# A Perceiver kernel on one core: the last experts' input made apart from its block, the last recurrence in other memory, and its end in two halves

## Chip, core and metric

The kernel runs on one core of one Trainium2 chip. The metric is the device time of one execution in microseconds (us), lower is better. The engines are named as in the profile: PE is TensorE (PEld its weight loads), DVE is VectorE, ACT is ScalarE, POOL is GpSimd, SP is SyncE, whose queue issues nearly all DMAs of the part in question. Each engine works through its own list of instructions in order. The lists are made when the kernel is built, and they interleave parts that the program writes one after the other: in the trace the input of block 2's experts is made in the middle of `recur(3)`, which stands before it in the program. So the order of the program works as a priority, not as a sequence.

## What is computed

64 sequences of 32 tokens with 256 channels (2048 tokens, float32) go through two layers, each with an attention part, a recurrent part and a feed-forward part, each added to the token. The change touches the last two parts of the second layer: the recurrence (a selective state-space model with 512 channels and 16 states) and the dense mixture of 8 experts.

```python
def _L1_attn_ref(x, ...):                      # x is normalised by the caller
    residual = x
    xz = x @ in_proj_w.T + in_proj_b
    x_main, z = jnp.split(xz, 2, axis=-1)
    xc = silu(causal_conv4(x_main) + conv_b)
    ssm = xc @ x_proj_w.T + x_proj_b
    B_param, C_param = ssm[..., :16], ssm[..., 16:32]
    delta = softplus(ssm[..., -1:])
    A = -jnp.exp(A_log)
    def step(h, ts):
        dt, B_t, C_t, x_t = ts
        h = jnp.exp(A[None] * dt[:, :, None]) * h + dt[:, :, None] * B_t[:, None, :] * x_t[:, :, None]
        return h, jnp.einsum('bdn,bn->bd', h, C_t) + D * x_t
    _, ys = lax.scan(step, h0, xs)
    y = (ys * silu(z)) @ out_proj_w.T + out_proj_b
    r = y + residual
    return layernorm(r) * ln_gamma + ln_beta

def _L1_ffn_ref(x, ...):                       # x is normalised by the caller
    logits = rms(xf @ gate_w.T + gate_b) * rms_w
    g = top_1(softmax(logits / 0.5))
    norm_g = g / (g + 1e-06)
    h = gelu(einsum('nd,edh->neh', xf, w1) + b1)
    y = einsum('neh,ehd->ned', h, w2) + b2     # all 8 experts, every token
    return (y * norm_g[:, None, None]).sum(axis=1)

x = x + _L1_attn_ref(_layernorm(x), ...)
x = x + _L1_ffn_ref(_layernorm(x), ...)
```

## The kernel before

The tokens stand in four blocks of 512, `k.x[0..3]`, each as four tiles of 128 tokens by 256 channels. `layers` (from L1233) runs six stages over them. The second layer's parts are `s3`, attention, by tiles of 128 tokens, called as `on(n, ...)`; `ahead`, `gates` and `recur` of `_stage4`, the recurrence, by blocks; and `s5` of `_stage5`, the experts, by blocks. Towards its end the program reads: attention for the last tiles (`on(6)`, `on(2)`, `on(4)`) with `ahead(2)`, `recur(1)` and `gates(2)` among them, then `s5(0)`, `ahead(3)`, `recur(2)`, `gates(3)`, `s5(1)`, `recur(3)`, `s5(2)`, `s5(3)`.

**The recurrence.** `ahead(b)` normalises the block, transposes it into `xT` (tag `xT4`, one buffer), makes the convolved channels `xc` (later `y`), sends B, C and the step through DRAM (`rows`) and turns the step into `dt` by a softplus of nine operations on ACT and DVE (L1059 to L1067). `gates(b)` makes `zs`, the gate, from the same `xT4` (L1075). `recur(b, v)` first multiplies `y` by `dt` (`dtx`, half on DVE, half on POOL, L1083). Then it goes over 16 states; for each, SP fetches one row of B and one of C to all partitions (`bc`, 512 KB, L1089), and for each half of the channels POOL makes `g` = dtx times B (L1092), ACT the decay `h` = exp(A dt) into a bank of PSUM (tag `h`, two banks, L1096), DVE runs the scan in place (L1097) and multiplies by C into `hc` (L1098), and POOL adds `hc` to `y` (L1103). `bc`, `g` and `hc` have two buffers each in the pool `wk`. After the states POOL multiplies `y` by the gate (L1106); then, tile by tile, the residual and `bout` are put into `xe` (L1110, L1111), PE projects `y` (`outps`, in the same two banks, L1114), DVE adds, and after all four tiles come the moments and a reciprocal root (`_rsqrt`: three operations on DVE, L84 to L87, and 12 Newton steps on POOL, L89 to L92), and gamma, beta and the sum into `x` on POOL (L1119 to L1121).

**The experts.** `block(b)` of `_stage5` has a head and a body. The head (L1152 to L1192): moments, `_rsqrt`, normalised tiles `xn5` (one buffer), transposes into `t_ps` (tag `u`, the one bank that `up` also uses), a copy to `xT5` (one buffer), the gate's logits `lg_ps` (L1166, same bank), and a softmax that ends in `gt`. The body (L1194 on) goes over 32 slices of 128 hidden channels, four for each expert: `up` (L1207, two matmuls into the one bank), an evacuation with the bias on ACT (L1209), and after four of them one gelu over the expert's `hid` (L1211, two buffers); the products with the second weights, `acc` (L1215), run one expert behind, into two banks. In the trace one matmul of this kind leaves two records, so a slice is four records of `up` and four of `acc`. Each expert's weights come on SP's queue (L1202, L1203, 512 KB each, two buffers each). At the end `acc` goes to `res` (L1220, in the buffer of `xT5`), is transposed back (`rT`, L1227, in the bank of `up`), multiplied by the gate and added to `x` into `o5` (L1228, in the buffer of `xn5`), and written out in two halves (L1230).

PSUM has eight banks here: two for attention, two `h`, one for projections (`psp`), one `u` (`psu`), two `acc`.

Of the kernel before, what the change touches and what calls it, by code (L numbers as in the profile page):

```python
# [8 lines left out]
F32 = mybir.dt.float32  # L9
# [6 lines left out]
P = 128  # L16
# [59 lines left out]
def _rsqrt(k, out, parts, tag, pool=None):  # L76


    nc, pool, f = k.nc, pool or k.small, out.shape[-1]
    n = out.shape[0]  # L80
    v, r, t = (pool.tile([P, f], F32, name=f"rs_{q}", tag=f"rs_{q}{tag}")[:n] for q in "vrt")
    at = 0
    for in_, scale, eps in parts:
        nc.vector.tensor_scalar(v[:, at : at + in_.shape[-1]], in_, scale, eps, ALU.mult, ALU.add)  # L84
        at += in_.shape[-1]
    nc.vector.tensor_scalar(r.bitcast(I32), v.bitcast(I32), 1, None, ALU.logical_shift_right)
    nc.vector.tensor_scalar(r.bitcast(I32), r.bitcast(I32), -1.0, 1597463007.0, ALU.mult, ALU.add)  # L87
    for step in range(3):
        nc.gpsimd.tensor_tensor(t, r, r, ALU.mult)  # L89
        nc.gpsimd.tensor_tensor(t, t, v, ALU.mult)  # L90
        nc.gpsimd.tensor_scalar(t, t, -0.5, 1.5, ALU.mult, ALU.add)
        nc.gpsimd.tensor_tensor(out if step == 2 else r, r, t, ALU.mult)  # L92
# [13 lines left out]
def _stats(k, tiles, tag, pool=None):  # L106

    mv = _moments(k, tiles, tag, pool)
    rstd = (pool or k.small).tile([P, len(tiles)], F32, name="rstd", tag=f"rstd{tag}")
    _rsqrt(k, rstd, [(mv[:, :, 1], 1.0, LN_EPS)], tag, pool)  # L110
    return mv, rstd
# [859 lines left out]
def _stage4(k, w, wk):  # L971
# [105 lines left out]
    def recur(b, v):  # L1077
        xs = [k.x[b][:, j, :] for j in range(4)]
        dt, y = v.dt, v.y
        dtx = wk.tile([P, C, BT], F32, name="dtx", tag="dtx", bufs=1)  # L1080
# [6 lines left out]
        for n in range(N):  # L1087
            bc = wk.tile([P, 2, BT], F32, name="bc", tag="bc", bufs=2)
            nc.sync.dma_start(bc, bc_rows[n].partition_broadcast(P))  # L1089
            for c2 in range(0, C, 2):  # L1090
                g = wk.tile([P, 2, BT], F32, name="g", tag="g", bufs=2)
                nc.gpsimd.tensor_tensor(g, dtx[:, c2 : c2 + 2], bc[:, 0:1, :].to_broadcast([P, 2, BT]), ALU.mult)  # L1092
                hc = wk.tile([P, 2, BT], F32, name="hc", tag="hc", bufs=2)
                for c in range(2):
                    h = ph([P, BT], "h")
                    nc.scalar.activation(h, dt, AF.Exp, scale=A[:, c2 + c, n : n + 1])  # L1096
                    nc.vector.tensor_tensor_scan(h, h, g[:, c, :], 0.0, ALU.mult, ALU.add)  # L1097
                    nc.vector.tensor_tensor(hc[:, c, :], h, bc[:, 1, :], ALU.mult)  # L1098
                if n == 0:

                    for c in range(c2, c2 + 2):
                        nc.scalar.activation(y[:, c, :], y[:, c, :], AF.Copy, scale=_chan(k, "L1_attn_D", c))
                nc.gpsimd.tensor_tensor(y[:, c2 : c2 + 2], y[:, c2 : c2 + 2], hc, ALU.add)  # L1103

        for c2 in range(0, C, 2):
            nc.gpsimd.tensor_tensor(y[:, c2 : c2 + 2], y[:, c2 : c2 + 2], v.zs[:, c2 : c2 + 2], ALU.mult)  # L1106
        xn = wk.tile([P, 4, D], F32, name="xe4", tag="hc", bufs=2)
# [9 lines left out]
        for j in range(4):  # L1117
            _norm(k, xn[j], xn[j], mv, rstd, j)
            nc.gpsimd.tensor_tensor(xn[j], xn[j], gamma, ALU.mult)  # L1119
            nc.gpsimd.tensor_tensor(xs[j], xs[j], beta, ALU.add)  # L1120
            nc.gpsimd.tensor_tensor(xs[j], xs[j], xn[j], ALU.add)  # L1121

# [6 lines left out]
def _stage5(k, w, out):  # L1129
# [12 lines left out]
    def ps(shape, name):  # L1142
        return k.psu.tile(shape, F32, name=name, tag="u")
# [7 lines left out]
    def block(b):  # L1151
        xs = [k.x[b][:, j, :] for j in range(4)]  # L1152
        mv, rstd = _stats(k, xs, "5")
        xT = k.wk5.tile([P, 2, BT], F32, name="xT5", tag="xT5", bufs=1)
        for j2 in range(0, 4, 2):
            xn = k.wk5.tile([P, 2, D], F32, name="xn5", tag="xn5", bufs=1)
            t_ps = ps([P, 2, 2 * P], "t_ps")
            for j in range(2):
                _norm(k, xn[:, j, :], xs[j2 + j], mv, rstd, j2 + j)
                for c in range(2):  # L1160
                    nc.tensor.transpose(t_ps[:, c, j * P : (j + 1) * P], xn[:, j, c * P : (c + 1) * P], k.ident)
            nc.scalar.copy(xT[:, :, j2 * P : (j2 + 2) * P], t_ps)
        lg_ps = ps([P, 4, E], "lg_ps")
# [28 lines left out]
        nc.vector.tensor_tensor(gt, gt, gn, ALU.mult)  # L1192

        acc = [k.psacc.tile([P, BT], F32, name="acc", tag="acc") for _ in range(2)]  # L1194
# [23 lines left out]
        res = k.wk5.tile([P, 2, BT], F32, name="res", tag="xT5", bufs=1)  # L1218
        for o in range(2):
            nc.scalar.activation(res[:, o, :], acc[o], AF.Identity, bias=b2s[:, o : o + 1])  # L1220
        for j2 in range(0, 4, 2):
            rT = ps([P, 2, D], "rT")
            t = k.wk5.tile([P, 2, D], F32, name="o5", tag="xn5", bufs=1)
# [8 lines left out]
    return block  # L1232


def layers(k, out):
# [11 lines left out]
    left0, left, right, right2 = ExitStack(), ExitStack(), ExitStack(), ExitStack()  # L1247
    k.lent = False
    with left0:
# [11 lines left out]
        k.wk3 = pool("wk3", 2)  # L1261
# [7 lines left out]
    with right, left:  # L1269
# [26 lines left out]
        s5 = _stage5(k, w5, out)  # L1296
        k.wk5 = pool("wk5", 2)
        on(6, True)
# [5 lines left out]
        s5(0)  # L1304
# [3 lines left out]
        s5(1)  # L1308
        recur(3, v[3])
        s5(2)  # L1310
        s5(3)
# [81 lines left out]
```

## Time and profile before

| what | value |
|---|---|
| median of 3 runs | 2078.18 us (2077.95 to 2079.32) |
| the profiled execution | 2077.47 us |
| its span, first to last instruction | 2075.5 us |
| mean granted TensorE clock | 0.826 |
| attention's last softmax row (L891) | starts at 1585.8 us |
| recurrences, start of the first g and of the last (L1092) | 773.2 and 997.2; 1123.4 and 1329.6; 1414.2 and 1638.8; 1704.8 and 1855.7 us |
| experts, block 0 | first up 1094.1, res 1410.0 us |
| block 1 | first up 1463.5, res 1734.2 us |
| block 2 | first up 1767.4, res 1925.4 us |
| block 3 | first up 1943.1, res 2064.7 us |

All times in the lower part are counted from the start of the span. The costliest groups of the page (line, engine, operation, tiles, shape, count, then busy time and mean length in ns, then the idle time just before them and what ended most of it) are those of the recurrence and the experts:

```profile
L1092 POOL TENSOR_TENSOR g<-dtx,bc 128x1024 f32<-128x1024 f32 x128 | 300.5, 2354 | 132.5 <-DVE h L1097 68.1
L1097 DVE TENSOR_TENSOR_SCAN h<-h,g 128x512 f32<-128x512 f32 x256 | 307.4, 1218 | 62.9 <-ACT h L1096 43.1
L1103 POOL TENSOR_TENSOR xc<-xc,hc 128x1024 f32<-128x1024 f32 x128 | 301.3, 2358 | 36.8 <-DVE hc L1098 22.9
L1207 PE MATMUL up<-xT,w 128*128 128x512 f32 x512 | 283.6, 670 | 38.9 <-ACT hid L1209 38.3
L1215 PE MATMUL acc<-hid,w 128*128 128x512 f32 x512 | 259.5, 630 | 27.2 <-ACT hid L1211 27.2
L1209 ACT ACTIVATE hid<-up,chan 128x512 f32<-128x512 f32 x128 | 87.4, 683 | 142.6 <-PE up L1207 142.4
```

The mean matmul length here is that of overlapping instructions and of two clocks; where PE is dense and the granted clock is 1.0, four records of `up` take 1.72 us in the chain.

### The profile page before, as it was taken

Reading aid. Unit: us, or ns where it says so; the run is one execution under the profiler, and the core shown is the slowest. Engines: PE = TensorE matmul, PEld = TensorE weight load, DVE = VectorE, ACT = ScalarE, POOL = GpSimd, SP = SyncE. Lnnn points to the kernel's source line nnn. Section 1 sums busy time; section 2 is a strip of 40 time slices with the busy share of each in tenths; the row PEclk is TensorE's granted clock in tenths of the full one; section 3 lists DMA queues with packets and bytes.
Section 4 is the critical chain, followed back from the end, with each engine's and each line's share of the span. In section 5 each row is a group of like instructions: output and inputs, shape, how many; then the busy total and the mean of one; then the engine's idle time right before and its main releaser. Section 6 shows DMA issues by size and latency. Waiting matters only on the chain. (4 is left out here: it accounts for less than half of the span.)

```text
span 2075.5 us, 20210 instructions
## 1 busy us (share of the span) xinstructions
PE 1616.5 (78%) x6323; PEld 823.7 (40%) x6323; DVE 1365.0 (66%) x2419; ACT 985.7 (47%) x2142; POOL 1074.2 (52%) x1221
## 2 busy tenths in 40 slices
PE   4676957669979888766888888787698674779798
PEld 3333524325645433433444344344343231234343
DVE  4488586765574559889765788757897758772100
ACT  3454343304535264444447676556476464553232
POOL 5444646413241316676633777734777759893000
PEclk9686867879989997555788899896699886999799
DMA  7654233200001012121101233111222113222121
GB/s 231 228 190 143 92 100 115 82 22 21 21 21 43 20 35 64 31 62 51 41 31 58 81 102 102 40 45 54 61 69 70 55 47 92 80 81 72 40 81 41
DMA packets 88378, 151.25 MB, mean 73 GB/s; under 512 B 7740, under 2 KB 52300, under 8 KB 86224
## 3 DMA queue, kind: packets, MB, share of 16 engines
q1 hardware_dynamic: 85428, 148.75, 23.6%
q10 hardware_dynamic: 2844, 1.22, 0.3%
q8 instruction: 50, 0.82, 0.2%
q14 instruction: 56, 0.46, 0.1%
HBM read 139.03 MB, written 10.92 MB: 72 GB/s over the span
## 5 line engine op out<-in xcount | busy, mean ns | idle before, releaser
L1092 POOL TENSOR_TENSOR g<-dtx,bc 128x1024 f32<-128x1024 f32 x128 | 300.5, 2354 | 132.5 <-DVE h L1097 68.1
L1097 DVE TENSOR_TENSOR_SCAN h<-h,g 128x512 f32<-128x512 f32 x256 | 307.4, 1218 | 62.9 <-ACT h L1096 43.1
L1103 POOL TENSOR_TENSOR xc<-xc,hc 128x1024 f32<-128x1024 f32 x128 | 301.3, 2358 | 36.8 <-DVE hc L1098 22.9
L1207 PE MATMUL up<-xT,w 128*128 128x512 f32 x512 | 283.6, 670 | 38.9 <-ACT hid L1209 38.3
L1215 PE MATMUL acc<-hid,w 128*128 128x512 f32 x512 | 259.5, 630 | 27.2 <-ACT hid L1211 27.2
L1096 ACT ACTIVATE h<-dt,A 128x512 f32<-128x512 f32 x256 | 172.9, 693 | 156.0 <-DVE hc L1098 155.8
L891 ACT ACTIVATE p<-sc,nm 128x256 f32<-128x256 f32 x256 | 117.7, 472 | 120.9 <-DVE nm L887 107.0
L1098 DVE TENSOR_TENSOR hc<-h,bc 128x512 f32<-128x512 f32 x256 | 169.5, 678 | 2.7 <-POOL xc L1103 1.0
L880 PE MATMUL sc<-kT,qm 32*128 32x256 f32 x512 | 145.1, 492 | 29.6 <-DVE od L920 21.4
L89 POOL TENSOR_TENSOR rs_t<-rs_r 128x4 f32<-128x4 f32 (+4 forms) x174 | 39.2, 228 | 246.5 <-DVE rs_r L87 233.1
L1207 PEld LDWEIGHTS up<-xT,w 128*128 128x128 f32 x512 | 98.1, 208 | 163.5 <-issue 87.1
L630 PE MATMUL weps<-we,xT 128*128 128x512 f32 x256 | 148.3, 705 | 14.8 <-DVE x L626 7.4
L1215 PEld LDWEIGHTS acc<-hid,w 128*128 128x128 f32 x512 | 98.7, 202 | 148.4 <-issue 102.9
L1209 ACT ACTIVATE hid<-up,chan 128x512 f32<-128x512 f32 x128 | 87.4, 683 | 142.6 <-PE up L1207 142.4
L906 PE MATMUL pt_ps<-ident,p 128*128 128x128 f32 x512 | 96.3, 322 | 36.6 <-ACT p L891 27.2
L880 PEld LDWEIGHTS sc<-kT,qm 32*128 32x128 f32 x512 | 85.5, 229 | 80.8 <-DVE od L920 35.0
L1228 DVE SCALAR_TENSOR_TENSOR o<-rT,gt,x 128x256 f32<-128x256 f32 x16 | 7.6, 477 | 164.7 <-PE rT L1227 158.4
L885 DVE TENSOR_REDUCE nm<-sc 128x2 f32<-128x512 f32 x128 | 86.0, 682 | 35.4 <-PE sc L880 34.8
L906 PEld LDWEIGHTS pt_ps<-ident,p 128*128 128x128 f32 x512 | 66.7, 162 | 90.3 <-ACT p L891 48.5
L908 ACT COPY pt<-pt_ps 128x512 f32<-128x512 f32 x128 | 74.4, 586 | 59.0 <-PE pt_ps L906 58.4
L530 POOL TENSOR_TENSOR kk<-kk 128x512 f32<-128x512 f32 x32 | 34.1, 1072 | 110.0 <-ACT kk L529 107.2
L247 POOL TENSOR_TENSOR cT<-cT,scb 128x2056 f32<-128x2056 f32 x16 | 73.2, 4575 | 27.6 <-PE sc L258 15.6
(390 smaller groups left out, 3203.3 us busy)
## 6 DMA issues: line engine op xcount, KB each, us to landing
bc<-rows SPq DMA_DIRECT2D x64, 512.0 KB
w<-in_L_ffn_w_dram SPq DMA_DIRECT2D x64, 512.0 KB
cT<-in_ctxT_dram SPq DMA_DIRECT2D x16, 1028.0 KB
cq<-cq SPq DMA_DIRECT2D x32, 514.0 KB
cn<-in_ctx_dram SPq DMA_DIRECT2D x64, 256.0 KB
scb<-scales SPq DMA_DIRECT2D x16, 514.0 KB
kb<-steps SPq DMA_DIRECT2D x16, 514.0 KB
x<-in_x_dram SPq DMA_DIRECT2D x4, 512.0 KB
```

Source lines behind the costliest of these rows:

```text
L630: nc.tensor.matmul(ps, xT[:, c, r], we[:, c, e : e + 2, :], start=c == 0, stop=c == 1)
L880: nc.tensor.matmul(sc[h][:, f, :], qm[r, e + f].rearrange("p l n g -> p (l n g)"), kTs[e][r, f, :], start=True, stop=True,)
L891: nc.scalar.activation(w_[:, f, h - h0, :], sc[h][:, f, :], AF.Exp, bias=nm[:, e + f, h : h + 1], accum_out=sm[:, e + f, h : h + 1],)
L906: nc.tensor.transpose(pt_ps[:, h, m, :], ws[e, hp][:, f, h, m * P : (m + 1) * P], k.ident)
L1092: nc.gpsimd.tensor_tensor(g, dtx[:, c2 : c2 + 2], bc[:, 0:1, :].to_broadcast([P, 2, BT]), ALU.mult)
L1096: nc.scalar.activation(h, dt, AF.Exp, scale=A[:, c2 + c, n : n + 1])
L1097: nc.vector.tensor_tensor_scan(h, h, g[:, c, :], 0.0, ALU.mult, ALU.add)
L1098: nc.vector.tensor_tensor(hc[:, c, :], h, bc[:, 1, :], ALU.mult)
L1103: nc.gpsimd.tensor_tensor(y[:, c2 : c2 + 2], y[:, c2 : c2 + 2], hc, ALU.add)
L1207: nc.tensor.matmul(u, w1[e][:, c, q * P : (q + 1) * P], xT[:, c, :], start=c == 0, stop=c == 1)
L1209: nc.scalar.activation(hid[e][:, q, :], u, AF.Identity, bias=b1)
L1215: nc.tensor.matmul(acc[o], w2[e][:, q, o * P : (o + 1) * P], hid[e][:, q, :], start=n == H, stop=n == E * H + H - 1)
```

## The change

Five things change.

1. `block` is split into `head(b, mem)`, which makes `xT`, the logits and the gate, and `block(b, v)`, the body. The head's `t_ps` and `lg_ps` move from the bank of `up` to the two banks of tag `h`. Its `xT` comes from a pool that is handed in: `in5` (one buffer) for blocks 0 and 1, `late` (two buffers) for blocks 2 and 3.
2. The heads get places of their own in the program: head 0 before `on(6)`, head 1 right after the body of block 0, head 2 after `gates(3)` and before the body of block 1, head 3 after `recur(3)` and before the body of block 2.
3. The pool of attention, `wk3`, gets a stack of its own (`right3`) and is closed after the last `on`; `late` is opened in its place. `recur(3)` takes `bc`, `g` and `hc` from `late`, with three buffers each instead of two.
4. For block 3 alone, `recur` makes the residual (norm, `bout`, and beta into `x`) at its start, in the buffer of `xT4`, and ends in two halves of two tiles (`end`): four matmul groups into one bank, one add over both tiles, moments, `_rsqrt` with its Newton steps on DVE instead of POOL, and two DVE operations for each tile in place of one on DVE and two on POOL. Head 3 also takes its moments and reciprocal root by pairs, on DVE.
5. A block's `res` and output go to one tile `last` in a buffer of `hid`, with a place for each half of the output.

```diff
-def _rsqrt(k, out, parts, tag, pool=None):
+def _rsqrt(k, out, parts, tag, pool=None, eng=None):
...
+    eng = eng or nc.gpsimd
...
-        nc.gpsimd.tensor_tensor(t, r, r, ALU.mult)
+        eng.tensor_tensor(t, r, r, ALU.mult)
...
-    def recur(b, v):
+    def recur(b, v, mem=None):
         xs = [k.x[b][:, j, :] for j in range(4)]
         dt, y = v.dt, v.y
+        if b == NBLK - 1:
+            xn = residual(v, xs)
+        own, more = (mem, 1) if mem else (wk, 0)
...
-            bc = wk.tile([P, 2, BT], F32, name="bc", tag="bc", bufs=2)
+            bc = own.tile([P, 2, BT], F32, name="bc", tag="bc", bufs=2 + more)
...
-                g = wk.tile([P, 2, BT], F32, name="g", tag="g", bufs=2)
+                g = own.tile([P, 2, BT], F32, name="g", tag="g", bufs=2 + more)
...
-                hc = wk.tile([P, 2, BT], F32, name="hc", tag="hc", bufs=2)
+                hc = own.tile([P, 2, BT], F32, name="hc", tag="hc", bufs=2 + more)
...
+        if b == NBLK - 1:
+            for j2 in range(0, 4, 2):
+                end(v, xs, xn, j2)
+            return
...
+    def residual(v, xs):
+        xn = wk.tile([P, 4, D], F32, name="xr4", tag="xT4", bufs=1)
+        for j in range(4):
+            _norm(k, xn[:, j, :], xs[j], v.mv, v.rstd, j)
+            nc.gpsimd.tensor_tensor(xn[:, j, :], xn[:, j, :], bout, ALU.add)
+            nc.gpsimd.tensor_tensor(xs[j], xs[j], beta, ALU.add)
+        return xn
+
+    def end(v, xs, xn, j2):
+        ps = ph([P, 2, D], "outps")
+        for j in range(2):
+            for c in range(C):
+                at = slice((j2 + j) * P, (j2 + j + 1) * P)
+                nc.tensor.matmul(ps[:, j, :], v.y[:, c, at], wout[:, c, :], start=c == 0, stop=c == C - 1)
+        t = xn[:, j2 : j2 + 2, :]
+        nc.vector.tensor_tensor(t, ps, t, ALU.add)
+        mv, rstd = _stats(k, [t[:, j, :] for j in range(2)], "4e", wk, nc.vector)
+        for j in range(2):
+            x = xs[j2 + j]
+            nc.vector.scalar_tensor_tensor(t[:, j, :], t[:, j, :], mv[:, j, 0:1], gamma, ALU.subtract, ALU.mult)
+            nc.vector.scalar_tensor_tensor(x, t[:, j, :], rstd[:, j : j + 1], x, ALU.mult, ALU.add)
...
-    def block(b):
-        xs = [k.x[b][:, j, :] for j in range(4)]
-        mv, rstd = _stats(k, xs, "5")
-        xT = k.wk5.tile([P, 2, BT], F32, name="xT5", tag="xT5", bufs=1)
+    def head(b, mem):
+        v = Ctx()
+        xs = v.xs = [k.x[b][:, j, :] for j in range(4)]
+        pairs = b == NBLK - 1
+        if not pairs:
+            mv, rstd = _stats(k, xs, "5")
+        xT = v.xT = mem.tile([P, 2, BT], F32, name="xT5", tag="xT5")
...
-            t_ps = ps([P, 2, 2 * P], "t_ps")
+            t_ps = k.psh.tile([P, 2, 2 * P], F32, name="t_ps", tag="h")
+            if pairs:
+                mv, rstd = _stats(k, xs[j2 : j2 + 2], "5e", k.wk5, nc.vector)
...
-        lg_ps = ps([P, 4, E], "lg_ps")
+        lg_ps = k.psh.tile([P, 4, E], F32, name="lg_ps", tag="h")
...
+        v.gt = gt
+        return v
+
+    def block(b, v):
+        xs, xT, gt = v.xs, v.xT, v.gt
...
-        res = k.wk5.tile([P, 2, BT], F32, name="res", tag="xT5", bufs=1)
+        last = k.wk5.tile([P, 4, BT], F32, name="last", tag="hid")
+        res, outs = last[:, 0:2, :], last[:, 2:4, :].rearrange("p a (b d) -> p (a b) d", d=D)
...
-            t = k.wk5.tile([P, 2, D], F32, name="o5", tag="xn5", bufs=1)
+            t = outs[:, j2 : j2 + 2, :]
...
-        k.wk3 = pool("wk3", 2)
+        k.wk3 = opened(right3, "right")("wk3", 2)
...
-        s5 = _stage5(k, w5, out)
+        head, s5 = _stage5(k, w5, out)
         k.wk5 = pool("wk5", 2)
+        in5 = pool("in5", 1)
+        f = {0: head(0, in5)}
         on(6, True)
         v[2] = ahead(2)
         recur(1, v[1])
         gates(v[2])
         on(2, False)
         on(4, True, last=True)
-        s5(0)
+
+        right3.close()
+        late = opened(right, "right")("late", 2)
+        s5(0, f[0])
+        f[1] = head(1, in5)
         v[3] = ahead(3)
         recur(2, v[2])
         gates(v[3])
-        s5(1)
-        recur(3, v[3])
-        s5(2)
-        s5(3)
+        f[2] = head(2, late)
+        s5(1, f[1])
+        recur(3, v[3], late)
+        f[3] = head(3, late)
+        s5(2, f[2])
+        s5(3, f[3])
```

More of the change, by code (lines that the diff above doesn't have):

```diff
@@ L88, in _rsqrt @@
     for step in range(3):
-        nc.gpsimd.tensor_tensor(t, r, r, ALU.mult)
-        nc.gpsimd.tensor_tensor(t, t, v, ALU.mult)
-        nc.gpsimd.tensor_scalar(t, t, -0.5, 1.5, ALU.mult, ALU.add)
-        nc.gpsimd.tensor_tensor(out if step == 2 else r, r, t, ALU.mult)
+        eng.tensor_tensor(t, r, r, ALU.mult)
+        eng.tensor_tensor(t, t, v, ALU.mult)
+        eng.tensor_scalar(t, t, -0.5, 1.5, ALU.mult, ALU.add)
+        eng.tensor_tensor(out if step == 2 else r, r, t, ALU.mult)
 def _moments(k, tiles, tag, pool=None):
@@ L103, in _moments, with _stats @@
     return mv
-def _stats(k, tiles, tag, pool=None):
+def _stats(k, tiles, tag, pool=None, eng=None):
     mv = _moments(k, tiles, tag, pool)
     rstd = (pool or k.small).tile([P, len(tiles)], F32, name="rstd", tag=f"rstd{tag}")
-    _rsqrt(k, rstd, [(mv[:, :, 1], 1.0, LN_EPS)], tag, pool)
+    _rsqrt(k, rstd, [(mv[:, :, 1], 1.0, LN_EPS)], tag, pool, eng)
     return mv, rstd
@@ L1149, in _stage5 @@
     nc.vector.tensor_copy(b2s, bs_ps)
-    def block(b):
-        xs = [k.x[b][:, j, :] for j in range(4)]
-        mv, rstd = _stats(k, xs, "5")
-        xT = k.wk5.tile([P, 2, BT], F32, name="xT5", tag="xT5", bufs=1)
+    def head(b, mem):
[5 more added lines that the diff above has]
+        xT = v.xT = mem.tile([P, 2, BT], F32, name="xT5", tag="xT5")
         for j2 in range(0, 4, 2):
             xn = k.wk5.tile([P, 2, D], F32, name="xn5", tag="xn5", bufs=1)
-            t_ps = ps([P, 2, 2 * P], "t_ps")
+            t_ps = k.psh.tile([P, 2, 2 * P], F32, name="t_ps", tag="h")
+            if pairs:
+                mv, rstd = _stats(k, xs[j2 : j2 + 2], "5e", k.wk5, nc.vector)
             for j in range(2):
-                _norm(k, xn[:, j, :], xs[j2 + j], mv, rstd, j2 + j)
+                _norm(k, xn[:, j, :], xs[j2 + j], mv, rstd, j if pairs else j2 + j)
                 for c in range(2):
@@ L1230, in block @@
             nc.sync.dma_start(out[at : at + 2 * P, :].rearrange("(j p) d -> p j d", p=P), t)
-    return block
+    return head, block
 def layers(k, out):
@@ L1246, in layers @@
     psum = dict(space=bass.MemoryType.PSUM)
-    left0, left, right, right2 = ExitStack(), ExitStack(), ExitStack(), ExitStack()
+    left0, left, right, right2, right3 = (ExitStack() for _ in range(5))
     k.lent = False
@@ L1268, in layers @@
         s1(NBLK - 1)
-    with right, left:
+    with right, right3, left:
         pool = opened(left, "left")
```

## The prediction

> **What bounds the kernel now.** I read the engine shares, then the 40 slices, the chain that ended last, and at last tables by stage for the stretches where the chain shows a gap on TensorE.
>
> From the page: busy time, then the slices of TensorE, GpSimd and TensorE's granted clock.
>
> ```profile
> PE 1616.5 (78%) x6323; PEld 823.7 (40%) x6323; DVE 1365.0 (66%) x2419; ACT 985.7 (47%) x2142; POOL 1074.2 (52%) x1221
> PE   4676957669979888766888888787698674779798
> POOL 5444646413241316676633777734777759893000
> PEclk9686867879989997555788899896699886999799
> ```
>
> A slice is 51.9 us. In slices 34 to 36 (1713 to 1868) GpSimd (POOL) runs at 9, 8 and 9 tenths: the last recurrence. TensorE (PE) stands at 4, 7 and 7 there, and falls to 7 once more in the 38th (1920), where POOL does nothing. So the tail is a POOL-bound recurrence with PE part used, then experts on PE alone.
>
> The chain that ended last (start, length, what), where the experts' blocks 1, 2 and 3 meet:
>
> ```profile
> 1723.40 1.92 ACT hid L1211
> 1725.36 8.86 PE acc L1215 x14
> ...
> 1763.57 3.59 PE lg_ps L1166 x16
> 1767.43 3.80 PE up L1207 x4
> ...
> 1916.42 0.69 ACT hid L1209
> 1917.14 1.92 ACT hid L1211
> 1919.10 7.15 PE acc L1215 x16
> 1926.27 0.70 ACT res L1220
> 1928.91 2.15 DMA out_dram<-o
> 1932.76 2.14 DMA out_dram<-o
> 1935.59 1.10 PE t_ps L1161 x4
> 1937.41 1.13 PE t_ps L1161 x4
> 1939.20 3.60 PE lg_ps L1166 x16
> 1943.07 3.80 PE up L1207 x4
> ```
>
> A block's input (t_ps, lg_ps) is made only after the block before it has gone out: xT5 and xn5 have one buffer each, shared with res and o5, and t_ps sits in the one bank of `up`. Block 2's x is final at 1688.4 and its first up comes at 1767.4; block 3's is final at 1887.6 and its first up comes at 1943.1.
>
> Busy time by stage (stretch, length, PE, PEld, DVE, ACT, POOL, granted clock, DMA share, GB/s): last recurrence; gap between blocks 1 and 2; block 2 beside the recurrence; block 3 in its steady part.
>
> ```profile
> 1704.80:1870.50 165.70, 107.56 (x226) 44.54 (x224) 134.40 (x155) 84.39 (x112) 155.93 (x80) 0.83 0.28 80
> 1718.90:1767.40 48.50, 19.27 (x50) 9.68 (x48) 39.53 (x47) 19.30 (x27) 46.43 (x21) 0.62 0.37 98
> 1767.40:1870.60 103.20, 74.29 (x151) 29.14 (x151) 83.94 (x97) 54.92 (x70) 95.69 (x54) 0.93 0.25 77
> 1962.70:2065.60 102.90, 101.86 (x237) 44.80 (x237) 0.00 (x0) 33.16 (x37) 0.00 (x0) 1.00 0.18 56
> ```
>
> **Block 1.** Its x is ready at 1394.0 (rstd). Its first transposes come at 1433 and its first up at 1463.5. In its steady part (1463.5 to 1637) 96 up records went, 24 units of four, 7.2 us a unit. Now its xT waits only for block 0's last up (1383). The work from first norm to last lg_ps took 1935.03 to 1942.8, 7.8 us with the engines free; with gates(2) on PE and ACT I take 12. First up at 1406, 57 us or 8 units sooner, so its last up goes near 1640 and not at 1717. This costs nothing beside attention if PE has room: PE is busy 164.8 of the 200 us from 1400 to 1600, and 8 units need 8 x 3.44 = 27.5. DVE, which is busy 165.3 there, gets no more work than before. If there is no room, see the third rival.
>
> **Block 2.** Its rstd ends at 1693.8. The psh banks are free between the last outps (1676) and the first h (1706), so head(2) runs in that hole; its POOL part is two rsqrt, 24 operations of 0.28, of which 12 now lie inside the recurrence. The tiles from `late` wait for attention's last reader, which wrote x at 1636: no wait. First up near 1707. At the pace beside the recurrence, 80 records in 103.2 us, or 5.16 us a unit, 32 units end at 1872, the last acc some 10 us later. Were block 1 not early, 1719.5 + 165 = 1884.5, still ahead of block 3's input. So the 48.5 us gap closes, and block 2 ceases to set the end. head issues no DMA, and SP's queue keeps its counts (32 + 32 weight loads, 64 bc, 8 outputs).
>
> **The last recurrence** then sets it. POOL's waits around it, us, times, longest:
>
> ```profile
> POOL dtx L1083 <- DVE dt L1067: 7.5, 1, 7.5
> POOL xc L1103 <- DVE hc L1098: 4.9, 3, 3.3
> POOL g L1092 <- DVE h L1097: 2.7, 2, 2.1
> ```
>
> POOL is busy 155.9 of 165.7; third buffers of bc, g and hc can win 9.8 at most and 0 at least. I take 6, as most of the idle time is a wait for h or hc, which deeper g and hc hide. Against it: residual puts 8 adds of 0.73 on POOL (5.8 us) into the 7.5 us hole before dtx, but only after xT4's last reader (1696.6), so 0 to 6 of them are late; I take 2. Queued behind them are dtx and the first g, for which the scan waits. Block 2 now has 8 gelus inside the recurrence where 5 were; each holds ACT 1.28 + 1.91 + 1.28, and all of POOL's idle time over those five is 9.8, so three more cost 0 to 6: I take 2. Net -2: the last product ends at 1868.5, before 1870.5.
>
> The SBUF — State Buffer page of the Trainium skill (Who interferes with whom) says that a VectorE instruction with two SBUF inputs and a GpSimd one that reads SBUF shut each other out for a whole instruction. By that, residual's adds could also hold up each of the three softplus steps before dt by 0.73, and the time would be 2 us above the one below. The trace half agrees: conv steps took 0.87 to 1.10 beside POOL's adds at 1667 and 0.73 to 0.75 without them at 1674.
>
> **The end by two tiles.** outps: the first pair 1.8 us after POOL, the second 5.5 after (24 records took 5.45). Then DVE per pair: add 0.7 (between L859's 0.67 and twice L1115's 0.42), stats 1.22, three seeds 0.6, 12 Newton steps 2.5 (0.205 each from DVE's L84 to L87; 3.4 at POOL's 0.28), four scalar_tensor_tensor 1.8 (0.37 half of L1038, 0.48 L1228), so 6.8; head(3) per pair 1.22 + 0.6 + 2.5 + 0.74 = 5.0. Two pairs 23.6 (22 to 28), on DVE alone, which then has nothing else. 1868.5 + 1.8 + 23.6 = 1893.9, and with transposes, copy, lg_ps (1.1 + 0.6 + 0.6 + 3.6 + 0.3) the first up at 1900.1. Before, rstd stood at 1892.3, so the new end by itself brings about 0; what brings the gain is that xn5, xT5 and the bank no longer wait for block 2's output.
>
> **Sum.** Block 3's first up 1943.1 to 1900.1: -43.0. From there to the end 132.4, less the second output pair's wait for the first pair's DMA (2.3 at 2070.49), as `outs` has a place for each. `last` takes a buffer of hid; block 2 is out by then, so no wait; if it were not, hid waits for the output to land, 8.8 us after acc. Span 2075.5 - 45.3 = 2030.2; the profiled execution took 2077.47, 1.97 more: 2032.2. Its own time lies 0.7 below the median of 2078.18, so I forecast **2033 us**.
>
> Block 3's first three ups took 3.80 each after a pause of PE, later ones 1.98. The TensorE: Matmul & The Clock Gate page of the Trainium skill (What's actually happening) gives half clock after an idle window of some 3.4 us. By that rule, were block 2's last accs to run into block 3's ups, the estimate would be 3 x 1.8 = 5.5 us lower.
>
> **Rivals.**
> Experts stay late (10%): the order is fixed at build time, and block 2's matmuls may still be queued to end at 1916.4. Then only the joint to block 3 closes: 16 acc records and 4 ups share PE for 14 us, evacuation and gelu 2.6, a hid wait of 4: first acc of block 3 at 1937 for 1962.7, with the output 28 us: 2050. For it: PE waited 36.8 us for ACT's hid after 1600. Against: those waits are short, 22 of them.
> Attention later (10%): block 1's 8 units push attention one for one, 27.5 us: 2060. For it: PE is in order. Against: 35 us idle there, and DVE is the fuller engine.
> It does nothing (4%): heads queued where they were; only the output's 2.3 is won: 2076.
> Slower (10%): SP's queue is in order, and bc stands behind weight loads that wait for a w1 buffer. Three bc cover 3 x 9.4 = 28 us of POOL; a wait of 49.5, the longest for a w1 in the whole run, leaves POOL 21 us dry; three of them cost 64: 2097. It decides from waits over 28 us. Against: the longest in the last recurrence was 24.5, with one visible bc wait of 1.1 on POOL.
>
> **How the numbers follow.** The forecast has 66%, with its own range 2019 to 2047 (all idle time won and nothing lost: -8, warm PE -5; residual and gelus at 6 each, no buffers, DVE at 28: +14 or +15). With the first two rivals 86%; the range 2017 to 2064 holds them. A change under 0.2% (4 us) can't be told from none: faster 0.86, same 0.04, slower 0.10.
>
> **What will show it.** Right: t_ps of block 2 before 1710, up of block 2 before 1725, no long PE gap until block 2 ends, then a pause of PE until lg_ps near 1896, chain through POOL g and xc. Wrong: dtx or attention's last x later than in the old trace, POOL under 9 tenths in the recurrence, SP waits over 28 us, block 2 still running when lg_ps of block 3 is done.

## The result and the profile after

The changed kernel takes 2053.51 us (median of 4, 2049.10 to 2055.91), the kernel before it, run beside it, 2078.75; the ratio is 0.9872, with a 95% interval of 0.9856 to 0.9888. So it is 25 us faster, where 45 were forecast.

From the page of the changed kernel: busy time, then the slices of TensorE, GpSimd and TensorE's granted clock.

```profile
PE 1618.9 (79%) x6323; PEld 819.6 (40%) x6323; DVE 1367.5 (67%) x2475; ACT 983.5 (48%) x2142; POOL 1062.7 (52%) x1189
PE   4775967759979888765788969878879677688898
POOL 5344656423142306776641776771477766998000
PEclk9677867879989998556689779988789889899999
```

TensorE's work is the same (1618.9 us for 1616.5) in a span of 2051.2 for 2075.5. A slice is now 51.3 us. GpSimd stands at 6 in slice 34 (1692 to 1743) and at 9, 9 and 8 in the next three, where it stood at 9, 8 and 9 in slices 34 to 36: the last recurrence is denser, but begins later.

The chain that ended last, from the start of the last recurrence to block 3's first up:

```profile
1722.87 2.30 POOL g L1096
1725.17 0.73 POOL xr L1137
1725.90 0.74 POOL x L1138
...
1730.79 2.32 POOL g L1096
...
1757.51 3.79 PE up L1250 x4
1761.39 0.70 ACT hid L1252
...
1909.43 1.82 PE acc L1258 x4
1911.25 0.81 PE lg_ps L1205 x8
...
1917.84 1.16 ACT last L1264 x2
1919.05 0.34 PE rT L1271
...
1922.46 0.49 DVE last L1272
1923.00 3.17 PE up L1250 x4
```

The last recurrence's first g starts at 1722.8, before at 1704.8, and the adds of residual stand between its first two g. Block 2's first up is at 1757.5, right behind block 1's output. Block 3's logits are done by 1912.1 (the second lg_ps), yet its first up waits until 1923.0: block 2's last acc, its result (ACT last) and the transposes rT come first. The joint between two blocks, which was to vanish, is short but still on the path.

By stage (stretch, length, then PE, PEld, DVE, ACT, POOL, granted clock, DMA share, GB/s): the last recurrence, the gap between blocks 1 and 2, block 2 beside the recurrence, block 3 in its steady part.

```profile
1722.80:1889.30 166.50, 124.27 (x264) 49.27 (x263) 126.32 (x150) 100.06 (x126) 160.72 (x87) 0.91 0.37 95
1740.80:1757.50 16.70, 3.01 (x8) 1.23 (x8) 15.92 (x22) 7.15 (x12) 13.35 (x7) 0.66 0.34 78
1757.50:1860.70 103.20, 85.54 (x176) 32.44 (x176) 83.04 (x94) 67.26 (x86) 103.20 (x45) 0.96 0.45 110
1942.20:2042.20 100.00, 99.00 (x232) 43.64 (x231) 0.00 (x0) 31.92 (x34) 0.00 (x0) 1.00 0.18 58
```

GpSimd is busy for 160.7 of 166.5 us in the last recurrence (155.9 of 165.7 before) and for all of the 103.2 us beside block 2. TensorE's gap between blocks is 16.7 us, before 48.5. GpSimd's waits from just before the recurrence to its end (us, times, longest):

```profile
POOL dtx L1087 <- DVE dt L1068: 3.7, 1, 3.7
POOL g L1096 <- DVE h L1101: 2.4, 1, 2.4
POOL g L1096 <- DVE lg L1221: 1.4, 1, 1.4
POOL xc L1107 <- DVE gn L1229: 1.0, 1, 1.0
```

Only 4.8 us are left behind dtx. Two of the three waits are for VectorE's small instructions of block 2's gate, which now lies inside the recurrence.

The places that the prediction named, from the traces of four kernels (the last two are experiments 5 and 6 below):

| us | before | after | block 0's bank put back | blocks 0 and 1 as before |
|---|---|---|---|---|
| block 0's result (ACT) | 1410.0 | 1447.2 | 1407.3 | 1404.7 |
| ups in 1400 to 1450 | 0 | 4 | 21 | 12 |
| block 1's result | 1734.2 | 1749.8 | 1679.3 | 1731.9 |
| block 2's first up | 1767.4 | 1757.5 | 1702.7 | 1739.7 |
| last recurrence, first g | 1704.8 | 1722.8 | 1719.6 | 1721.6 |
| its last product ends | 1870.5 | 1889.3 | 1872.4 | 1874.4 |
| block 2's result | 1925.4 | 1917.8 | 1884.9 | 1903.2 |
| block 3's first up | 1943.1 | 1923.0 | 1898.0 | 1908.5 |
| span | 2075.5 | 2051.2 | 2024.8 | 2036.4 |

The executions are not in step to begin with: the first recurrence, which the change does not touch, starts at 773.2, 775.3, 770.4 and 767.9, so differences of a few us between columns say nothing. The column "after" holds the surprise: block 0's result is 37 us *later* than before, and block 1's 16 us later, although block 1's input is made earlier than it was.

### The profile page after: what moved, and what is told of

It is laid out like the page before. It is cut to its first block, busy times and chain, and to the rows that moved or that the text cites. A ratio compares the mean times of both kernels' runs of the same rounds, so it can differ in the third digit from the quotient of the medians.

```text
span 2051.2 us, 20219 instructions
## 1 busy us (share of the span) xinstructions
PE 1618.9 (79%) x6323; PEld 819.6 (40%) x6323; DVE 1367.5 (67%) x2475; ACT 983.5 (48%) x2142; POOL 1062.7 (52%) x1189
## 5 line engine op out<-in xcount | busy, mean ns | idle before, releaser
L1258 PE MATMUL acc<-hid,w 128*128 128x512 f32 x512 | 269.1, 647 | 21.1 <-ACT hid L1254 21.1
L1272 DVE SCALAR_TENSOR_TENSOR last<-rT,gt,x 128x256 f32<-128x256 f32 x16 | 7.6, 478 | 125.4 <-PE rT L1271 125.4
L915 PE MATMUL oT_ps<-pt,v 128*32 128x128 f32 x1024 | 74.5, 313 | 18.2 <-ACT pt L909 18.1
```

The lines of the kernel that those rows point to most:

```text
L1258: nc.tensor.matmul(acc[o], w2[e][:, q, o * P : (o + 1) * P], hid[e][:, q, :], start=n == H, stop=n == E * H + H - 1)
```

## The experiments

The times are medians; ratios are to the kernel before, run beside them.

**1. Block 1's input late** (on the changed kernel; the bank of `up` is psu, tag "u").

```
-        f[1] = head(1, in5)
         v[3] = ahead(3)
...
         f[2] = head(2, late)
+        f[1] = head(1, in5)
         s5(1, f[1])
```

and its t_ps and lg_ps in the bank of `up`.

> Block 1's input is made where it was before the change: behind the recurrence of block 2, in the bank of `up`; all else as changed. Theory E (experts' chain: block 1 gained nothing from its early input, since its ups only fill what attention leaves of TensorE; the end is set by the row of blocks 1, 2 and 3): block 1's result stays within 8 us of 1749.8, block 3's first up within 5 us of 1923.0, time 2049 to 2058. Theory H (the early input pushed block 2's part ahead of its recurrence 13 us back, and with it both last recurrences, and this sets the end): last recurrence's first g back from 1722.8 to 1704 to 1712, block 3's first up near 1908 to 1913, time 2038 to 2044. The prediction's step (block 1 wins 8 units from its early input): block 1's result 30 us or more later, time 2075 or more.

Measured: 2157.13 us, ratio 1.0378 (1.0348 to 1.0408). The up matmuls in two stretches of this kernel (length, PE, PEld, clock, DMA share, GB/s):

```profile
1600.00:1650.00 50.00, 0.00 (x0) 0.00 (x0) 0.50 0.12 32
1700.00:1750.00 50.00, 16.68 (x20) 5.17 (x20) 0.67 0.09 21
```

The edit did more than it was meant to. xn5 has one buffer, taken in program order; block 1's input now stood behind block 2's, which waits for the recurrence of block 2 to end. So there was no up at all from 1450 to 1700. It is no test of the prediction's step (experiment 6 is), but it decides against theory H: block 0's result stayed at 1446.0 and the last recurrence at 1724.8 with block 1's input out of the way.

**2. No third buffers** (on the changed kernel).

```
-        own, more = (mem, 1) if mem else (wk, 0)
+        own, more = wk, 0
```

> The changed kernel with two buffers of bc, g and hc in the last recurrence, as in the others. The prediction's step (third buffers win 6 of the 9.8 us in which GpSimd idled): from first g to the end of the last product 166.5 becomes 170 to 173, time up by 4 to 6 if the recurrence sets the end, by 0 to 2 if the experts' chain does. Theory E: the recurrence ends up to 6 us later but block 3's first up stays within 3 us of 1923.0, time within 3 us of the changed kernel's.

Measured: 2054.31 us, ratio 0.9891 (0.9865 to 0.9916), no difference from the changed kernel. From first g (1722.3) to the end of the last product (1890.3) 168.0 us, for 166.5 with them (the prediction's step asked for 170 to 173), and GpSimd's waits inside are 6.0, for 4.8. The third buffers win 1.2 to 1.5 us on GpSimd, and these are not on the path.

**3. The result's transposes in another bank** (on the changed kernel).

```
-            rT = ps([P, 2, D], "rT")
+            rT = k.psp.tile([P, 2, D], F32, name="rT", tag="p") if b else ps([P, 2, D], "rT")
```

> The transposes of a block's result take the bank that the recurrences' projections used (free after the last gates), not the bank of `up`, for blocks 1 to 3; all else as changed. Theory E: block 2's first up moves from 1757.5 to 1738 to 1750 and block 3's from 1923.0 to 1908 to 1915 (block 3's input is there at 1909.5 to 1912.0), time 2038 to 2046. Theory R (the last recurrence and its end set block 3's start, the joints cost nothing): block 3's first up after 1919, time within 4 us of 2053.5.

Measured: 2040.78 us, ratio 0.9816 (0.9794 to 0.9838), 12.7 below the changed kernel. TensorE at the joint of blocks 2 and 3:

```profile
1914.05 1.10 PE L1258 MATMUL acc<-hid,w 128*128 128x512 f32 x2
1914.99 0.27 PE L1271 MATMUL rT<-ident,last 128*128 128x128 f32 x1
1915.10 1.02 PE L1250 MATMUL up<-xT,w 128*128 128x512 f32 x2
```

Block 2's last acc, the first transpose of its result and block 3's first ups now follow each other without a pause, and a pair of ups takes 1.02 where four took 3.17 after the pause. Block 3's first up is at 1915.1 for 1923.0. At the other joint block 2's first four up records come at 1731.7 for 1757.5, but the next at 1756.5: TensorE waits there for block 1's result on ScalarE. So in the changed kernel the experts' row set the end, not the last recurrence.

**4. Block 0's input as before the change** (place and bank).

```
-        f = {0: head(0, in5)}
...
+        f[0] = head(0, in5)
         s5(0, f[0])
```

and its t_ps and lg_ps in the bank of `up`.

> Block 0's input is made right before its experts, in the bank of `up`, as before the change; all else as changed. Theory H0 (block 0's early input and experts take TensorE's turns before block 2's part ahead of its recurrence: ssm at 1401.4, before 1387.0): recurrence of block 2 starts near 1414 to 1418 again, the last one at 1705 to 1712, time 2040 to 2053. Theory H (block 1's early input alone did that): both starts stay within 4 us of 1427.5 and 1722.8, time within 4 us of 2053.5.

Measured: 2027.62 us, ratio 0.9751 (0.9730 to 0.9773), 25.9 below the changed kernel and more than either theory gave. The recurrence of block 2 starts at 1413.2 again, as theory H0 has it; the last one still at 1721.2, as it does not.

**5. Only block 0's bank** (its place stays early).

```
-            t_ps = k.psh.tile([P, 2, 2 * P], F32, name="t_ps", tag="h")
+            t_ps = ps([P, 2, 2 * P], "t_ps") if b == 0 else k.psh.tile([P, 2, 2 * P], F32, name="t_ps", tag="h")
```

and lg_ps alike.

> Block 0's input keeps its new place (ahead of attention's six steps and the recurrence of block 1), but its transposes and logits go back to the bank of `up`; all else as changed. In the run with place and bank both old, block 0's result came at 1409.0, that of the changed kernel at 1447.2. Theory bank (the two banks of the recurrence's h, lent to block 0's input, are what delays block 0): result of block 0 at 1405 to 1415, time 2024 to 2032. Theory place (the early place alone changes the order in which TensorE takes block 0's matmuls and attention's): result of block 0 at 1440 to 1452, time 2048 to 2056.

Measured: 2028.89 us, ratio 0.9748 (0.9728 to 0.9769). The bank alone does it; the early place costs nothing. The up matmuls of the changed kernel (columns as in experiment 1):

```profile
1075.00:1225.00 150.00, 36.96 (x52) 11.20 (x52) 0.78 0.21 62
1225.00:1375.00 150.00, 34.06 (x64) 10.65 (x64) 0.87 0.24 71
1400.00:1450.00 50.00, 2.15 (x4) 0.68 (x4) 0.80 0.25 70
```

and of this one:

```profile
1075.00:1225.00 150.00, 37.99 (x60) 12.66 (x60) 0.87 0.25 66
1225.00:1375.00 150.00, 36.07 (x64) 10.99 (x64) 0.87 0.24 67
1400.00:1450.00 50.00, 14.59 (x21) 4.66 (x21) 0.83 0.19 64
```

In the first 150 us block 0 gets 60 ups through for 52 and then holds its lead; in the third stretch there are 21 ups, nearly all block 1's, for 4 that are still block 0's. The granted clock of the first stretch differs too (0.78 for 0.87); the edit does not touch it, and no run parts what the order costs from what the clock costs.

The order in which TensorE takes its instructions does differ, from block 0's logits on. In the changed kernel:

```profile
1087.82 0.96 PE L1205 MATMUL lg_ps<-w_L_ffn_gate_wT,xT 128*128 128x8 f32 x8
1090.56 1.10 PE L1250 MATMUL up<-xT,w 128*128 128x512 f32 x2
```

and in this one:

```profile
1084.85 2.61 PE L1205 MATMUL lg_ps<-w_L_ffn_gate_wT,xT 128*128 128x8 f32 x16
1091.31 3.78 PE L1250 MATMUL up<-xT,w 128*128 128x512 f32 x4
```

With the two banks of h the logits come in two parts with attention's work between them (the second part starts at 1089.65), and the first ups in twos with attention between them; with the one bank of `up` the 16 logits stand together and so do the first four ups. By the tile they write, all 6323 of TensorE's records stand in one order in this kernel and in experiment 4's, and this is the order of the kernel before up to block 1's transposes at 1392.7. So the early place not only costs nothing, it left TensorE's order as it was.

The end of this kernel, on TensorE:

```profile
1896.27 1.88 PE L1205 MATMUL lg_ps<-w_L_ffn_gate_wT,xT 128*128 128x8 f32 x8 [0.67 <-ACT xT L1201]
1898.00 3.76 PE L1250 MATMUL up<-xT,w 128*128 128x512 f32 x4
```

lg_ps ends and block 3's ups follow: now the last recurrence and its end set block 3's start, at 1898.0.

**6. Blocks 0 and 1 as before the change.** As 4, and block 1's input, in the bank of `up`, behind gates(v[3]) and ahead of block 2's.

```
-        f[1] = head(1, in5)
...
         gates(v[3])
+        f[1] = head(1, in5)
         f[2] = head(2, late)
```

> Blocks 0 and 1 both have their inputs made where and in the bank in which they were before the change (block 1's ahead of block 2's, so that its xn5 does not wait for that one); block 2's and 3's as changed. The prediction's step (block 1's early input brings its row 57 us forward): block 1's first up goes from about 1418 to near 1463 and its result from 1680.7 to 1725 or later; block 2, which starts behind it, ends near 1915 and not at 1886.5, block 3's first up near 1920 and not at 1899.7, time 2042 to 2052. Rival (the room beside attention is the same for whatever block is there, so block 1 catches up): block 1's result within 10 us of 1680.7 and time within 5 us of 2027.6.

Measured: 2043.36 us, ratio 0.9812 (0.9792 to 0.9832), 15.7 above experiment 4. Block 1's first up is at 1432.8, not near 1463; its result goes to 1731.9 and block 3's first up to 1908.5, with its logits done at 1897.5: without block 1's early input (place and bank were undone together) the row of experts sets the end again.

**7. The old end of the last recurrence** (on experiment 4; residual and end left away, the four tiles end together as in the other blocks).

```
-        if b == NBLK - 1:
-            xn = residual(v, xs)
...
-        if b == NBLK - 1:
-            for j2 in range(0, 4, 2):
-                end(v, xs, xn, j2)
-            return
```

> Block 0's input at its old place and bank; the last recurrence ends as the others do (no adds ahead of it, no end by two tiles: four tiles together, Newton steps on GpSimd, gamma, beta and x on GpSimd); block 3's input still in two pairs. The prediction's step (the new end by itself brings about 0): the adds' 7.9 us ahead of the last recurrence go, the end takes 21.8 to the last x as before, block 3's first up 1895 to 1903, time 2023 to 2031. Rival (the new end is worth more: from the last product to block 3's first up it took 25.5 us, before it would have been some 30, and the adds are hidden by the wait for dt): block 3's first up 1904 or later, time 2032 to 2038.

Measured: 2033.54 us, ratio 0.9762 (0.9735 to 0.9789); the interval holds experiment 4's ratio. By its time this is the rival's case (2032 to 2038), by block 3's first up, 1901.7 for 1899.5, the prediction's (1895 to 1903). Two parts work against each other: from the last product to that first up it is 29.3 us for 25.4, so the new end wins 3.9; without the adds the first g comes 82.9 us after the last g of the recurrence before, for 85.3, so the adds cost 2.4. The new end is worth about 2 us by the traces; the medians differ by 5.9, which the noise of this run (2024.69 to 2037.53) does not settle.

**8. Residual's adds on VectorE** (on experiment 4).

```
-            nc.gpsimd.tensor_tensor(xn[:, j, :], xn[:, j, :], bout, ALU.add)
-            nc.gpsimd.tensor_tensor(xs[j], xs[j], beta, ALU.add)
+            nc.vector.tensor_tensor(xn[:, j, :], xn[:, j, :], bout, ALU.add)
+            nc.vector.tensor_tensor(xs[j], xs[j], beta, ALU.add)
```

> Block 0's input at its old place and bank, and the eight adds that the change puts ahead of the last recurrence run on VectorE and not on GpSimd. With them on GpSimd they took 1710.69 to 1718.81 there, just ahead of dtx, with dt final at 1716.6. Theory P (these adds hold up dtx): first g from 1721.2 to 1716 to 1718, time 2022 to 2025. Theory D (dt itself is late there, since the softplus stands between the gates and the table loads of block 2's input, and the adds only fill the wait): first g and time within 2 us of 1721.2 and 2027.6.

Measured: 2025.70 us, ratio 0.9737 (0.9719 to 0.9755), the same as experiment 4. The first g came at 1726.1, in an execution that was 6 us behind from the first recurrence on. From the last g of the recurrence before to this first g it took 84.2 us for 85.3. In time this is theory D's case, but its reason does not hold: the adds do hold up dt. A step of the softplus in experiment 4, then in this one:

```profile
1711.48 1.21 DVE L1066 TENSOR_TENSOR e__11121<-e__11121,u__11122 128x512 f32<-128x512 f32 x1
1717.05 0.69 DVE L1066 TENSOR_TENSOR e__11121<-e__11121,u__11122 128x512 f32<-128x512 f32 x1
```

Beside GpSimd's adds two of these steps took 1.21 us, without them 0.69 and 0.68, and dt is final 77.9 us after the last g of the recurrence before, where it was 80.7. Of these 2.8 us 1.1 reach the first g: the adds, and a step of block 2's gate that took 2.30 us, now stand ahead of VectorE's half of dtx, which starts 4.9 us after dt is final, and GpSimd waits 3.6 us for it.

**9. Block 0's input in a third bank**, that of the projections (on the changed kernel; lg_ps alike).

```
+            t_ps = k.psp.tile([P, 2, 2 * P], F32, name="t_ps", tag="p") if b == 0 else k.psh.tile([P, 2, 2 * P], F32, name="t_ps", tag="h")
```

> The changed kernel, but block 0's input goes through the one bank of the recurrences' projections, neither through the bank of `up` (2028.9 with that) nor through the two of h (2053.5). Theory U (what block 0 lost is that its input no longer stands in its own row's bank, so the fixed order takes TensorE's instructions in another sequence): result of block 0 at 1430 to 1455, time 2045 to 2060. Theory B (the banks of h are the cost, since the recurrence of block 0 or 1 waits for them): result of block 0 at 1405 to 1415, time 2024 to 2034.

Measured: 2054.92 us, ratio 0.9887 (0.9856 to 0.9917), block 0's result at 1444.0. That is theory U's number, but not for its reason. The projections hold this bank, and block 0's transposes come at 1114.3 here, 36 us later than in the changed kernel (1078.5); from then on its row is not slow. From block 0's first up to its last it takes 291.2 us here, 288.8 in experiment 5 and 324.9 in the changed kernel. Over all kernels of this study it is 286.5 to 291.2 in the ten that make block 0's input in one bank, whichever, and 324.9 to 327.9 in the four that make it in the two banks of h (the changed kernel and experiments 1 to 3). So a bank other than its own row's does not by itself slow the row, and a block 0 that ends late, here for another reason, gives the changed kernel's time.

Theory B's reason, a recurrence that waits for the banks of h, does not hold either. In experiment 5 and in the changed kernel the input is made at the same time (transposes from 1073.7 and 1078.5, logits done by 1087.5 and 1090.7), between two recurrences (last g of the one at 999.1, first g of the next at 1125.8 in the changed kernel), where nobody else uses the banks of h; and the next recurrence is no slower for it (203.9 us from first to last g, for 206.4). What differs is the sequence in which TensorE takes its instructions, as experiment 5 shows.

**10. Experiments 3 and 5 together** (the diffs of both).

> Block 0's input in the bank of `up`, at its early place, and the transposes of the results of blocks 1 to 3 in the bank of the projections. With block 0's input in the bank of h the second of these won 12.7 (2053.5 to 2040.8). Theory E (there the row of experts' blocks set block 3's start; with block 0 mended, the last recurrence and its end set it, logits done at 1897.8 and first up at 1898.0): time within 4 us of 2028.9, first up within 4 us of 1898.0. Rival (the joint costs the same wherever it lies): time 2014 to 2019.

Measured: 2031.12 us, ratio 0.9769 (0.9732 to 0.9806), no gain over 2028.89. What was worth 12.7 us on the changed kernel is worth nothing here, since the joint is off the path. (The first up is at 1903.4, outside of the 4 us, in an execution that was 4.6 us behind experiment 5's at the start of the first recurrence and 11 at the next.)

**11. Block 2's input behind the last recurrence in the program**, in the bank of `up`, with 10.

```
-        f[2] = head(2, late)
         s5(1, f[1])
         recur(3, v[3], late)
+        f[2] = head(2, late)
         f[3] = head(3, late)
```

> Block 0's and block 2's inputs in the bank of `up`; block 2's is made behind the last recurrence in the program and so comes after it in rank; results' transposes in the bank of the projections. Theory E (the last recurrence sets block 3's start, and what delays its dt, final at 1716.6 for 1701.2 before the change, is that block 2's input came ahead of gates and softplus on TensorE, ScalarE and VectorE): first g from 1719.6 to 1708 to 1715, block 3's first up 1887 to 1894, time 2016 to 2024. Rival (block 2 now starts so late that it sets block 3's start): block 2's result after 1900, block 3's first up after 1903, time 2032 or more.

Measured: 2029.64 us, ratio 0.9769 (0.9738 to 0.9800). Neither theory: first g at 1721.6, block 2's result at 1886.1, as if nothing had been moved. The built order places block 2's transposes ahead of three of the four gate projections all the same. Place and bank were changed together here; that the place alone need not decide the order is shown by experiments 4 and 5, which differ in block 0's place and have one order on TensorE.

**12. Block 2's input in the bank of the gates' projections**, with 10, so that it has to stand behind them; its place is that of the changed kernel, and its t_ps and lg_ps are tiles of k.psp with tag "p", as block 0's in 9. What is to be undone, on TensorE in the kernel of experiment 4:

```profile
1695.04 1.11 PE L1200 MATMUL t_ps<-ident,xn 128*128 128x128 f32 x4 [7.31 <-DVE xn L116]
1696.38 3.13 PE L1014 MATMUL inps<-xT,w_L_attn_in_projT 128*128 128x512 f32 x4
```

TensorE waits 7.3 us for the norm ahead of block 2's transposes, with projections of the gates (inps) behind them; ScalarE, in order too, gets to the softplus only after it has read one of these.

> Block 0's input in the bank of `up`; block 2's input, and the transposes of the results of blocks 1 to 3, in the bank of the projections, so that block 2's transposes stand behind the four projections of the gates on TensorE (before, they stood ahead of three of them and TensorE waited 7.3 us there for the norm). Theory E (the last recurrence and its end set block 3's start, and its dt is late since the gates and the softplus wait behind block 2's input): ScalarE reaches the softplus at 1692 to 1696 in place of 1701, first g from 1721.6 to 1708 to 1715, block 3's first up 1886 to 1894, time 2015 to 2024. Rival (the softplus comes late for another reason, or the eight adds and the rsqrt take up what is won): first g after 1718, time 2025 to 2032.

Measured: 2024.77 us, ratio 0.9725 (0.9699 to 0.9751). ScalarE is at the softplus at 1691.8 and the first g comes at 1711.1, as theory E has it. From the last g of the recurrence before to this first g it is 74.6 us, for 84.0 in experiment 10, which differs in block 2's bank alone. But of these 10 us only 3 reach the end of the last product (1871.6 for 1874.5 in experiment 11, which differs only in the place and bank of block 2's input), and block 3's first up, at 1896.8, and the time miss theory E's ranges (1886 to 1894, 2015 to 2024): the last section shows where the rest went. It is the fastest kernel of the study by its median, 28.7 below the changed one, but its interval overlaps those of experiments 4, 5, 7, 8, 10 and 11.

## Why the prediction came out as it did

**The direction was right, the size was not, and the mechanism was right in part.** The measured 2053.5 lies outside the forecast's own range (2019 to 2047), near the first rival's 2050. The joint between blocks 2 and 3 became shorter, but in the changed kernel the experts' row, not the last recurrence, still sets the end. The step that failed is the one on block 1: "Now its xT waits only for block 0's last up (1383)." It took block 0 as it stood. head(0) also moved, to an earlier place and to other banks, and that edit I did not cost at all. In the changed kernel block 0's last up starts at 1415.5, not at 1383, and block 1's first at 1462.7, not at 1406. The banks alone are worth 24.6 us (2053.5 for 2028.9, experiment 5). With it undone the forecast holds closely: block 3's first up 1898.0 for the predicted 1900.1, time 2028.9 for 2033. That closeness is in part luck: the last product ends 3.9 us later than predicted (1872.4 for 1868.5), and the stretch from there to block 3's first up is 6.0 us shorter (25.6 for 31.6).

**How 40 us of block 0 become 25 at the end.** Block 0's last up comes at 1415.5 and its result at 1447.2, 40 us later than in experiment 5; block 1 has no up before 1450, and its result comes 70 us later; block 2's first up comes 55 later, and its result, behind a denser row, 33 later; block 3's first up 25. The recurrence of block 2 begins 16 later too (1427.5 for 1411.5). The changed kernel's execution was 5 us behind already at the start of the first recurrence (775.3 for 770.4).

**Block 1.** Its early input was costed at 57 us for its own row. In experiment 5 its last up starts at 1641.6, near the predicted 1640, and undoing place and bank of its input costs 15.7 us at the end (experiment 6).

**Block 2.** "head(2) runs in that hole" (1694 to 1706): in the changed kernel its transposes come at 1716.1 and its first up at 1757.5, since block 1's output, whose transposes share the bank of `up`, stood ahead of it; with block 0 mended the transposes start at 1693.7 and the first up at 1702.7 (predicted 1707). That "block 2 ceases to set the end" was wrong for the changed kernel (experiment 3: 12.7 us) and right for experiment 5 (experiment 10: nothing).

**The last recurrence.** Its start was taken as unchanged but for 2 us. It starts 18 us late; in experiment 5 still 15, with dt behind gates that queue behind block 2's input (experiment 12 wins 10 us there). The 2 us taken for residual's adds were right for experiment 4, where they cost 2.4 (experiment 7); in the changed kernel all eight stand between the first two g and take 5.6 us of GpSimd's time there. "I take 6" for the third buffers was too much: 1.2 to 1.5 in the changed kernel (experiment 2). In experiment 5 GpSimd's waits are gone altogether (152.6 busy of 152.8 from first g to the last product, 165.7 before), and block 2's twelve Newton steps, 3.4 us, no longer lie in it, so its last product is only 2 us later than before for a start 15 us later; whether the third buffers have a part in that was not tried.

**The end by two tiles.** Predicted 1.8 + 23.6 + 6.2 from the last product to the first up; it took 25.6 in experiment 5 (1872.4 to 1898.0), and 22.7 to the last logits in the changed kernel. The term that was too large is VectorE's 23.6: from the first pair's add to the last norm it is 15.6 us in the changed kernel and 17.8 in experiment 5, where the two pairs' instructions alternate in the trace and fill each other's gaps. That the new end "by itself brings about 0" was right within 2 us by the traces of experiment 7; the medians leave up to 6 open.

**The tail** from block 3's first up was to be 130.1; it is 128.2, and 126.8 in experiment 5. Two groups of four ups were slow (3.17 and 3.72, then 2.00), not three. The rule on the clock gate, cited from the Trainium skill (TensorE: Matmul & The Clock Gate, What's actually happening), gave faster ups if block 2's acc ran into them, and experiment 3's 1.02 a pair agrees.

**The rivals.** "Experts stay late" had the right place and almost the time (2050, block 2's matmuls ahead of block 3's), with a chance of 10%: too little. Its ground, an order fixed at build time, was the right one, but I applied it to block 2's queue alone and not to the first thing that the diff re-places, block 0. "Attention later" did not happen (its last x at 1638.8 for 1636.9). In the slower rival SP was to hold up bc: its longest wait for a weight buffer was 28.2 us, and GpSimd waited for no bc.

**What stays open.** The runs show that the two banks of h decide, and that TensorE's order differs from block 0's logits on while the input itself is not late. By which rule the build came to the worse order they do not show, nor how much of the slower row is the order and how much the lower granted clock in it.

## What to carry to other kernels

Where the instruction order is fixed at build time, an edit that only moves a tile to another memory bank may re-order everything behind it; look at when the *first* stage that the diff touches ends, before asking what the later ones win. A joint between two stages is worth its length only while it lies on the path: the same edit brought 12.7 us here and nothing on a base 25 us faster. And count what an instruction stands ahead of in an in-order queue: block 2's transposes, "in the hole", held up the gates and the softplus behind them.

## What the runs showed of the hardware

Small VectorE instructions can wait for a whole GpSimd one. VectorE, in experiment 12, at the start of the last recurrence:

```profile
1711.30 0.17 DVE L1218 TENSOR_REDUCE ms<-sq 128x4 f32<-128x32 f32 x1
1711.50 1.94 DVE L85 TENSOR_SCALAR rs_v<-ms 128x4 f32<-128x4 f32 x1
1713.48 2.27 DVE L87 TENSOR_SCALAR rs_r<-rs_v 128x4 int32<-128x4 int32 x1
1716.06 0.15 DVE L88 TENSOR_SCALAR rs_r<-rs_r 128x4 int32<-128x4 int32 x1
```

GpSimd in the same stretch, two g in one line:

```profile
1711.06 4.66 POOL L1096 TENSOR_TENSOR g<-dtx,bc 128x1024 f32<-128x1024 f32 x2
```

Two instructions on 128 x 4 elements took 1.94 and 2.27 us, where the third of the same kind took 0.15 between two g. The first ends at 1713.4 and the second at 1715.7, just as the two g do (1711.06 + 2.3 and + 4.66). The reduce over 128 x 32 took 0.17 in the middle of the first g and did not wait. The next of block 2's gate that met a g took 2.31 (lg, two inputs). Behind them waited the scan, and behind the scan GpSimd itself (2.0 us ahead of a product). Of the 10 us won at the start 7.5 were lost again: GpSimd's waits in this recurrence are 4.4, and the twelve Newton steps of 0.28 that now lie in it 3.4. The Trainium skill (SBUF — State Buffer, Who interferes with whom) names this lock: a VectorE instruction with two SBUF inputs, or a tensor_scalar in a two-port mode, and a GpSimd instruction that reads SBUF shut each other out for a whole instruction, while a reduce never contends. The trace agrees for the instruction with two inputs and for the reduce; that the two tensor_scalars ran in a two-port mode is not shown, only that they waited. The prediction had priced this rule at 2 us, on the adds of residual. There it acts too: two of the three softplus steps took 1.21 us beside the adds in experiments 4 and 5, for 0.69 and 0.68 without them in experiment 8. In the changed kernel the adds come after the softplus, whose three steps took 0.68 each. The larger price was on block 2's gate.
